# Four graph layers on one core: deferred loads, other turns, six exp buffers, and the MLP's second product by seven products

## The chip, the cores and the metric

The kernel runs on one core of one Trainium2 chip. The metric is the device time of one launch in microseconds (us), as a median over runs. The core's engines are named as in the profile: PE (TensorE, matrix products; PEld are its weight loads), DVE (VectorE), ACT (ScalarE), POOL (GpSimd), and SP (SyncE), which only issues DMAs here. Lines such as L521 are lines of the kernel before.

## The reference, cut to what matters

64 graphs of 256 nodes with 256 features pass four layers. After each layer the input is added and rows are normalised.

```python
# layer 0: 4 heads of 64, masked by adj
out = softmax(where(adj == 0, NEG, q @ k.T * 64**-0.5)) @ v
x = layernorm(x + layernorm(out @ Wo.T + bo) * gamma + beta)
# layer 1: 8 heads of 32 on the normalised rows themselves, then an MLP
normed = layer_norm(x, gamma1, beta1)
x1 = x + softmax(masked(normed @ normed.T * 32**-0.5)) @ normed
y = layer_norm(x1, gamma2, beta2)
x = layernorm(x + x1 + gelu(y @ W1 + b1) @ W2 + b2)      # W1 256x1024, W2 1024x256
# layer 2: scores from two vectors, leaky_relu, masked softmax, times x @ W
# layer 3: scores (x * a0) @ x.T, leaky_relu, masked softmax, times x
```

The product `gelu(...) @ W2` is the MLP's second product. Adjacency holds 0 and 1, is symmetric and has a full diagonal.

## The kernel before

The work runs in f32. `usual_input` does it all; at its end a flag tells whether the inputs had the properties that it relies on, and only if not, `any_input` computes everything again in a slower way. With these inputs it isn't entered.

**Groups and turns.** Two graphs are a group (G = 2, T = 512 rows), so there are 32 groups. `group(g)` is a generator: it loads x and adj, makes the mask, and runs layers 0 to 3; at each `yield` another generator may go on. The order of the program is that of the turns: the digits of `FIRST` name the groups that take the first turns; then, for each of 32 periods, the digits of `ORDER` name ages, where age a in period p is group p - a; the digits of `LAST` count back from the last group. In steady state groups of six ages are under way, and one leaves per period. `prepare`, which works out small constants (bop, the extra columns of wx, b2m, bounds), takes turns of its own beside group 0 from that group's turn `PREPARE` + 1 on.

**Engine order.** PE's instructions keep exactly the order of the program (`in_order` chains them). The other engines' instructions were set in an order of their own when the program was built; on the chip each engine runs its list in that order and waits for semaphores.

**What the steps put where.** Scores go into `ps` (PSUM, two buffers of 128x1024), ACT makes `e` by exp (L598), DVE multiplies by the mask (L600 for layer 0, L606 for layer 1, four of 256 columns for each e, with the row sums), PE multiplies e by the values (`pm<-e,v`, `pm<-e,z`). `e` has eight buffers. All other products go into `pm` (PSUM, four buffers of 128x512). Normalisation is bn_stats and bn_aggr on DVE (L537, L538), then two POOL instructions for the root (L540, L544), then DVE (L552). Layer 0 needs 1/sum along the other axis: `behind` writes zs to DRAM (`lines`, L719) and reads it back spread over partitions (`rr`, L721, two DMAs for each graph), all issued by SP; then DVE scales oT (L723), PE multiplies by WoT, and DVE's L730 and the norms follow, up to z. PE transposes z (L524) for layer 1.

**The MLP.** L779 is ACT's gelu into hT, laid out 128 x 8 x 512. `project` then computes, for each graph, a bias product (`b2m`, bf16, three rows that sum to b2 minus beta1) and, for both blocks of 128 rows, 8 matmuls with 128 rows of hT stationary and 256 columns of W2 moving; DVE's L692 adds `both` and takes the sum from PSUM into y. It yields after each block.

**Start.** SP issues, in this order: x and adj of group 0, WvT, WoT, the small constants, x and adj of group 1, W1, W2, adj of group 2, and then the first four DMA transposes (adjT, L888) that the mask (L891) needs. WqT, WkT, bq and bk are issued by ACT.

Of the kernel before, what the change touches and what calls it, by code (L numbers as in the profile page):

```python
# [8 lines left out]
F32 = mybir.dt.float32  # L9
# [4 lines left out]
ALU = mybir.AluOpType  # L14
AX = mybir.AxisListType

P = 128
N = 256
D = 256
NC = D // P  # L20
G = 2
QB = N // P
# [4 lines left out]
NF = DFF // P  # L27
# [6 lines left out]
AT_ONCE = 3  # L34


ORDER = "011225334342343542234235432323132121321132121"


FIRST = "3100000000021101000001010000010111"  # L40
LAST = ("001142322312324311231243212120210102100210100031121201213200120132101010010120100010101102"
        "01021000001000010010000")
PREPARE = 5

# [356 lines left out]
def usual_input(ctx: ExitStack, tc: tile.TileContext, a: dict, out: bass.AP, flag: bass.AP):  # L401
# [40 lines left out]
    def load_group(g):  # L442
        x0 = io.tile([P, TB, D], F32, name="x0")
        nc.sync.dma_start(x0, a["x"][g * G:(g + 1) * G].rearrange("b (q p) d -> p (b q) d", p=P))
        adj = io.tile([P, TB, N], I32, name="adj")
        nc.sync.dma_start(adj, a["adj"][g * G:(g + 1) * G].rearrange("b (q p) k -> p (b q) k", p=P))
        return x0, adj

    def load_rows(name, cols, queue=nc.sync):

        src = a[name]
        t = const.tile([P, src.shape[0] // P, cols], F32, name=name)
        queue.dma_start(t, src.rearrange("(c p) f -> p c f", p=P))
        return t

    def load_column(src, n, name, queue=nc.sync):

        t = const.tile([P, n // P], F32, name=name)
        queue.dma_start(t, src.rearrange("(c p) -> p c", p=P))
        return t  # L460

    setup = act.tile([P, NF, T], F32, name="setup", tag="hT", bufs=1).rearrange("p f t -> p (f t)")
# [1 line left out]
    def load_all(src, name, at=None):  # L464

        t = const.tile([P, D], F32, name=name) if at is None else setup[:, at:at + D]
        nc.sync.dma_start(t, src.unsqueeze(0).to_broadcast([P, D]))
        return t


    first = load_group(0)
# [1 line left out]
    wkT = load_rows("L0_gnn_WkT", D, nc.scalar)  # L473
    bq = load_column(a["L0_gnn_bq"], D, "bq", nc.scalar)
    bk = load_column(a["L0_gnn_bk"], D, "bk", nc.scalar)
    wvT = load_rows("L0_gnn_WvT", D)
    woT = load_rows("L0_gnn_WoT", D)
    bv = load_column(a["L0_gnn_bv"], D, "bv")
    bo = load_all(a["L0_gnn_bo"], "bo", 0)

    wx = const.tile([P, NC, D + 3], F32, name="wx")
    nc.sync.dma_start(wx[:, :, 0:D], a["L2_gnn_W"].rearrange("(c p) f -> p c f", p=P))
    a12 = setup[:, 768:1280].rearrange("p (s d) -> p s d", s=2)
    nc.sync.dma_start(a12, a["L2_gnn_a"].rearrange("(s f) o -> o s f", s=2).to_broadcast([P, 2, D]))
    beta0 = load_all(a["L0_gnn_beta"], "beta0")
    gamma0 = load_all(a["L0_gnn_gamma"], "gamma0")
    beta1r = load_all(a["L1_gnn_beta1"], "beta1r")
# [5 lines left out]
    beta2 = load_column(a["L1_gnn_beta2"], D, "beta2")  # L493
    b1 = load_column(a["L1_gnn_b1"], DFF, "b1")
    a0 = load_column(a["L3_gnn_a0"], D, "a0")
    second = load_group(1)
    w1 = load_rows("L1_gnn_W1", DFF)
    w2 = load_rows("L1_gnn_W2", D)

    wa1 = const.tile([P, 2, NC], F32, name="wa1")  # L500
    b2m = const.tile([P, D], BF16, name="b2m")
    onesb = const.tile([P, P], BF16, name="onesb")
# [17 lines left out]
    def matmul(*args, **kw):  # L520
        in_order(nc.tensor.matmul(*args, **kw))  # L521
# [60 lines left out]
    def scores(i, cs, qT, kT, mask, hd, scale, sums=None):  # L582

        m = P // hd
        es = []
        for c in cs:
            pss = [ps_s.tile([P, 2, QB * N], F32, name="ps") for _ in range(m // 2)]
            for kc in range(QB):  # L590
                for h in range(m):
                    r = h * hd
                    matmul(pss[h // 2][:, h % 2, kc * N:(kc + 1) * N],
                           kT[r:r + hd, c, i * N + kc * P:i * N + (kc + 1) * P],
                           qT[r:r + hd, c, i * N:(i + 1) * N], start=True, stop=True)
            for ps in pss:
                e = att.tile([P, 2, QB * N], F32, name="e", bufs=8)
                nc.scalar.activation(e, ps, AF.Exp, scale=scale)  # L598
                if sums is None:
                    nc.vector.tensor_tensor(e, e, mask.unsqueeze(1).to_broadcast([P, 2, QB * N]), ALU.mult)  # L600
                else:
                    for h in range(2):
                        for kc in range(QB):
                            k = slice(kc * N, (kc + 1) * N)
                            j = 2 * len(es) + h
                            nc.vector.scalar_tensor_tensor(e[:, h, k], e[:, h, k], 1.0, mask[:, k], ALU.mult, ALU.mult,  # L606
                                                           accum_out=sums[:, kc, c, j:j + 1])
                es.append(e)
        return es
# [63 lines left out]
    def project(dst, srcT, w, extra, row=None, gs=ALL):  # L673


        chunks = w.shape[1]
        for i in gs:
            pm = ps_m.tile([P, QB, D], F32, name="pm")
            if row is not None:
                matmul(pm, onesb, row.unsqueeze(1).to_broadcast([P, QB, D]), start=True, stop=False)  # L680
            for q in range(QB):
                t = i * QB + q
                for c in range(chunks):
                    matmul(pm[:, q, :], srcT[:, c, t * P:(t + 1) * P], w[:, c, :],
                           start=c == 0 and row is None, stop=c == chunks - 1 and (row is None or q == QB - 1))
                if chunks > NC:
                    yield
            o = dst[:, i * QB:(i + 1) * QB, :]
            if extra is None:
                nc.scalar.copy(o, pm)  # L690
            else:
                nc.vector.tensor_tensor(o, pm, extra[:, i * QB:(i + 1) * QB, 0:D], ALU.add)  # L692

    def layer0(g, x, mask):
        xT = transposed(x)
# [178 lines left out]
        return (yield from values_of(lambda i, kc, q: e[:, i, at[kc][q]:at[kc][q] + P], x, D, x, r_3[:, g], gs, last[:, g]))  # L874

    def group(g):
        x, adj = (first, second)[g] if g < 2 else load_group(g)
        yield
        adjb = io.tile([P, TB, N], BF16, name="adjb", bufs=1)
        nc.scalar.activation(adjb, adj, AF.Copy, accum_out=there[:, g:g + 1])  # L880
        nc.scalar.activation(adj.bitcast(F32), adj, AF.Square, bias=minus_half, accum_out=edges[:, g:g + 1])
        yield


        pt = io.tile([P, G, QB, N], BF16, name="adjT", bufs=1)
        for t in range(TB):
            i, q = divmod(t, QB)
            nc.sync.dma_start_transpose(pt[:, i, :, q * P:(q + 1) * P], adjb[:, t, :])  # L888
        yield
        mask = act.tile([P, G, QB * N], BF16, name="mask")  # L890
        nc.vector.scalar_tensor_tensor(mask.rearrange("p g k -> p (g k)"), pt.rearrange("p g k q -> p (g k q)"), 1.0,  # L891
                                       adjb.rearrange("p t k -> p (t k)"), ALU.mult, ALU.min,
                                       accum_out=both_ways[:, g:g + 1])
        xb, z = yield from layer0(g, x, mask)
        y, hT, both = yield from layer1(xb, z, mask)

        def others(gs):

            yield from project(y, hT, w2, both, b2m, gs)
# [12 lines left out]
        while parts:  # L912
            for r in parts[:turn // QB + 1]:
                if next(r, END) == END:
                    parts.remove(r)
            turn += 1
            yield

    def prepare():


        bvr = setup[:, 2560:2816].rearrange("p (c q) -> p c q", c=NC)
        nc.vector.tensor_copy(bvr, bv.unsqueeze(2).to_broadcast([P, NC, P]))
# [5 lines left out]
        yield  # L929
# [15 lines left out]
        for k in range(3):  # L945
            nc.vector.tensor_copy(part, left)
            nc.sync.dma_start(b2m[k:k + 1, :], part[0:1, :])
            if k < 2:
                nc.vector.tensor_tensor(left, left, part, ALU.subtract)

        yield

# [101 lines left out]
```

## Time and profile before

| | us |
|---|---|
| median of 10 runs (2661.74 to 2667.36) | 2665.37 |
| the profiled execution, its own time | 2668.45 |
| span of its instructions | 2666.6 |
| PE busy | 2591.1 |
| DVE busy | 1966.4 |
| ACT busy | 1293.2 |
| first mask (L891) starts at | 31.3 |
| mask to mask, from 217.9 to 2466.9 | 80.3 |

Durations below come from the one profiled execution. "Busy" is the union of an engine's instructions. A group line of the profile reads: line, engine, operation, written tile <- read tiles, shapes, count, then busy us and the mean ns of one, then the engine's idle time just before and what ended it. A timeline line reads: start, length, engine, line, operation, tiles, count, and in brackets the idle time before it. A product in f32 appears as two records on PE. Matmuls are pipelined, so the records of neighbours overlap, and the distance between starts is what they cost.

### The profile page before, as it was taken

To read this page: it belongs to the slowest core of one execution; us is meant where nothing else is said; L and a number is where in the kernel's file an instruction comes from. 1 tells how busy PE (TensorE), PEld (TensorE's weight loads), DVE (VectorE), ACT (ScalarE), POOL (GpSimd) and SP (SyncE) were. 2 spreads that over 40 slices of the span, in tenths; PEclk is the share of its full clock that TensorE was granted. 3 is DMA by queue.
4 is the path that set the end of the run, shared out by engine and by line. 5 is a ranking of instruction groups with operands and counts; after the bars stand their busy time and mean duration, and the time that the engine had idled before them with its cause. 6 is when DMAs were issued, how large, how long until landed. Compare 5 with 4: busy or idle time off the path is not lost.

```text
span 2666.6 us, 44866 instructions
## 1 busy us (share of the span) xinstructions
PE 2591.1 (97%) x16648; PEld 1767.3 (66%) x16648; DVE 1966.4 (74%) x6189; ACT 1293.2 (48%) x1995; POOL 587.5 (22%) x1139
## 2 busy tenths in 40 slices
PE   6899999999999999999999999999999999999996
PEld 3466667666666676666676666676676676676665
DVE  4667777777777777777777777777777777777774
ACT  3445545545544445545455545555444555444442
POOL 1112222212222212222222222222222222222221
PEclk8899999999999999999999999999999999999998
DMA  5001011100010110110110110010110110000000
GB/s 154 25 9 29 29 37 29 33 29 29 29 37 27 31 32 25 32 37 26 28 37 25 32 37 25 29 37 23 35 36 25 29 37 21 29 29 17 17 1 25
DMA packets 113728, 83.20 MB, mean 31 GB/s; under 512 B 44256, under 2 KB 113120, under 8 KB 113504
## 3 DMA queue, kind: packets, MB, share of 16 engines
q1 hardware_dynamic: 112416, 79.74, 10.1%
q8 instruction: 134, 2.20, 0.4%
q14 instruction: 90, 0.74, 0.1%
q10 hardware_dynamic: 1088, 0.53, 0.1%
HBM read 54.80 MB, written 17.04 MB: 27 GB/s over the span
## 4 chain that ended last, share of the span: by engine, by line
PE 72%; DVE 16%; POOL 8%; issue 2%; DMA 1%; SPq 1%; ACT 1%; DVEq 0%; ACTq 0%; POOLq 0%
PE pm L521 55%; PE ps L521 10%; PE pm L524 7%; POOL rstd L544 6%; DVE st L537 3%; DVE y L807 2%; DVE y L735 2%; DVE xn L552 2%; POOL ve L540 2%; DVE z L552 2%; DVE mv L538 1%; DVE y L734 1%; DVE xb L741 1%; DVE r L806 1%; SPq L888 1%
## 5 line engine op out<-in xcount | busy, mean ns | idle before, releaser
L606 DVE SCALAR_TENSOR_TENSOR e<-e,mask 128x256 f32<-128x256 f32 x1024 | 428.3, 485 | 130.0 <-ACT e L598 130.0
L598 ACT ACTIVATE e<-ps 128x1024 f32<-128x1024 f32 x384 | 372.2, 1021 | 197.5 <-PE ps L521 181.0
L521 PE MATMUL pm<-L_gnn_W,hT 128*128 128x256 f32 x2048 | 463.0, 379 | 0.0
L521 PE MATMUL pm<-xT,L_gnn_W 128*128 128x512 f32 x1024 | 455.8, 593 | 0.0
L521 PEld LDWEIGHTS pm<-L_gnn_W,hT 128*128 128x128 f32 x2048 | 384.5, 190 | 49.2 <-issue 0.7
L779 ACT ACTIVATE hT<-pm,b 128x512 f32<-128x512 f32 x256 | 177.2, 692 | 409.7 <-PE pm L521 409.7
L521 PEld LDWEIGHTS pm<-xT,L_gnn_W 128*128 128x128 f32 x1024 | 192.4, 191 | 204.0 <-issue 199.5
L537 DVE BATCH_NORM_STATS2 st<-y 128x6 f32<-128x256 f32 x768 | 301.8, 409 | 6.7
L544 POOL TENSOR_TENSOR rstd<-ve,mhalf 128x2 f32<-128x2 f32 (+1 forms) x384 | 298.0, 776 | 26.7
L552 DVE TENSOR_SCALAR xn<-y,mv,rstd 128x256 f32<-128x256 f32 x384 | 142.2, 412 | 177.4 <-POOL rstd L544 177.4
L540 POOL TENSOR_SCALAR ve<-mv 128x2 f32<-128x2 f32 x384 | 98.9, 258 | 757.7 <-DVE mv L538 757.2
L765 POOL TENSOR_TENSOR both<-y,xb 128x512 f32<-128x512 f32 x64 | 81.3, 1271 | 760.4 <-DVE y L764 760.4
L600 DVE TENSOR_TENSOR e<-e,mask 128x1024 f32<-128x1024 f32 x128 | 151.0, 1221 | 17.4 <-ACT e L598 17.4
L521 PE MATMUL ps<-xT 32*128 32x256 f32 x2048 | 151.8, 407 | 1.7 <-ACT e L598 1.5
L579 ACT ACTIVATE xT<-pm,beta,gamma 128x512 f32<-128x512 f32 x128 | 92.6, 771 | 113.3 <-PE pm L524 113.1
L521 PEld LDWEIGHTS ps<-xT 32*128 32x128 f32 x2048 | 95.0, 187 | 75.4 <-issue 66.4
L521 PE MATMUL pm<-e,z 128*32 128x256 f32 x2048 | 139.2, 387 | 0.1
L521 PE MATMUL pm<-L_gnn_WoT,oT 128*128 128x256 f32 x512 | 121.4, 391 | 13.2 <-DVE oT L723 13.2
L521 PE MATMUL pm<-e,v 128*32 128x256 f32 x2048 | 125.5, 386 | 5.6 <-DVE e L600 5.6
L521 PE MATMUL ps<-qT,kT 64*128 64x256 f32 x1024 | 128.0, 389 | 0.6 <-ACT e L598 0.6
L521 PE MATMUL pm<-xT,L_gnn_WqT 128*128 128x512 f32 x256 | 120.2, 613 | 3.4 <-ACT xT L577 3.4
L807 DVE SCALAR_TENSOR_TENSOR y<-pm,r,xn 128x256 f32<-128x256 f32 x256 | 121.2, 474 | 2.5
(136 smaller groups left out, 4064.5 us busy)
## 6 DMA issues: line engine op xcount, KB each, us to landing
x<-in_x SPq DMA_DIRECT2D x32, 512.0 KB
adj<-in_adj SPq DMA_DIRECT2D x32, 512.0 KB
rr<-lines SPq DMA_DIRECT2D x128, 128.0 KB
out<-xn SPq DMA_DIRECT2D x31, 512.0 KB
L_gnn_W<-in_L_gnn_W SPq DMA_DIRECT2D x2, 1024.0 KB
adjT<-adjb SPq DMA_TRANSPOSE x128
lines<-zs SPq DMA_DIRECT2D x64, 4.0 KB
out<-xn SPq DMA_DIRECT2D x2, 256.0 KB
```

Of the source, the lines that this page charges most:

```text
L521: in_order(nc.tensor.matmul(*args, **kw))
L524: in_order(nc.tensor.transpose(*args))
L537: nc.vector.bn_stats(st[:, q, :], src[:, t, 0:D])
L540: nc.gpsimd.tensor_scalar(ve[:, 0], mv[:, :, 1], EPS, None, ALU.add)
L544: nc.gpsimd.tensor_tensor(rstd, ve, mhalf[:, 0:k * QB].rearrange("p (k t) -> p k t", k=k), ALU.pow)
L552: nc.vector.tensor_scalar(dst[:, t, 0:D], src[:, t, 0:D], mv[:, q, 0:1], rstd[:, q:q + 1], ALU.subtract, ALU.mult)
L579: nc.scalar.activation(dst[:, c, on], pt[:, on], AF.Identity, bias=bias[:, c:c + 1], scale=scale[:, c:c + 1])
L598: nc.scalar.activation(e, ps, AF.Exp, scale=scale)
L600: nc.vector.tensor_tensor(e, e, mask.unsqueeze(1).to_broadcast([P, 2, QB * N]), ALU.mult)
L606: nc.vector.scalar_tensor_tensor(e[:, h, k], e[:, h, k], 1.0, mask[:, k], ALU.mult, ALU.mult, accum_out=sums[:, kc, c, j:j + 1])
L779: nc.scalar.activation(hT[:, f, :], pm, AF.Gelu, bias=b1[:, f:f + 1])
L807: nc.vector.scalar_tensor_tensor(y[:, t, :], po[:, 0:D], r, x[:, t, 0:D], ALU.mult, ALU.add)
```

## The change

**Seven products.** For every group but the last, `project` is replaced by `quarters` and `in_seven`. hT is taken as a 2 x 2 matrix of blocks (graph x half of the 1024), W2 as 2 x 2 (half of the 1024 x half of the columns). `quarters` forms three new sums of blocks in s1, s2 and s4 and one in place in hT; `prepare` forms four differences of W2's blocks once, in `wd`. Seven block products then take the place of eight, each 8 matmuls with 128 moving columns, accumulated in pa, px and py, and DVE adds them up in y. s1, s2 and s4 use the buffers of z, kT and qT.

**Loads.** What group 0's first steps don't need is put into the list `later` and issued on SP at the start of `prepare`. WvT goes to ACT's queue. Group 1 is loaded in its own turn.

**Turns and buffers.** FIRST, ORDER, LAST and PREPARE are other rows (36 first turns instead of 34; PREPARE 2 with four empty turns behind the loads). `e` has six buffers instead of eight.

```diff
-ORDER = "011225334342343542234235432323132121321132121"
-FIRST = "3100000000021101000001010000010111"
-LAST = ("001142322312324311231243212120210102100210100031121201213200120132101010010120100010101102"
-        "01021000001000010010000")
-PREPARE = 5
+ORDER = "001222533434324352334422132453233212211231312"
+FIRST = "000000110000021311001001010000001011"
+LAST = ("011142232321324122331102134212210110012020100031121210213011220010231011000011020010101020"
+        "11012000000100100010000")
+PREPARE = 2
...
+    later = []
+    def load(queue, to, of):
+        if queue:
+            queue.dma_start(to, of)
+        else:
+            later.append((to, of))
...
-    wvT = load_rows("L0_gnn_WvT", D)
+    wvT = load_rows("L0_gnn_WvT", D, nc.scalar)
...
-    second = load_group(1)
+    wd = const.tile([P, 4, NF // 2, P], F32, name="wd")
...
-                e = att.tile([P, 2, QB * N], F32, name="e", bufs=8)
+                e = att.tile([P, 2, QB * N], F32, name="e", bufs=6)
...
+    def quarters(hT):
+        a = [[hT[:, k * NF // 2:(k + 1) * NF // 2, i * N:(i + 1) * N] for k in range(2)] for i in range(G)]
+        s1 = act.tile([P, NF // 2, N], F32, name="s1", tag="z")
+        s2 = act.tile([P, NF // 2, N], F32, name="s2", tag="kT")
+        s4 = act.tile([P, NF // 2, N], F32, name="s4", tag="qT")
+        nc.vector.tensor_tensor(s1, a[1][0], a[1][1], ALU.add)
+        nc.vector.tensor_tensor(s2, s1, a[0][0], ALU.subtract)
+        nc.vector.tensor_tensor(a[1][0], a[0][0], a[1][0], ALU.subtract)
+        nc.vector.tensor_tensor(s4, a[0][1], s2, ALU.subtract)
+        return a, s1, s2, s4
+
+    def in_seven(dst, of, extra):
...
+        pa = ps_m.tile([P, QB, 2, P], F32, name="pm")
+        px = ps_m.tile([P, QB, 2, P], F32, name="pm")
+        product(pa[:, :, 0], a[0][0], quarter(0, 0))
+        w = att.tile([P, QB, P], F32, name="w", bufs=1)
+        nc.scalar.copy(w, pa[:, :, 0])
+        nc.vector.tensor_tensor(r1[:, :, 0], pa[:, :, 0], e1[:, :, 0], ALU.add)
+        matmul(px, onesb, rows, start=True, stop=False)
+        product(px[:, :, 0], a[1][1], wd[:, 3], False, False)
+        yield
+        product(px[:, :, 1], s1, wd[:, 0], False)
+        nc.vector.tensor_tensor(r2, px, e2, ALU.add)
+        nc.vector.tensor_tensor(r1[:, :, 1], px[:, :, 1], e1[:, :, 1], ALU.add)
+        product(pa[:, :, 1], s2, wd[:, 1])
+        nc.vector.tensor_tensor(w, w, pa[:, :, 1], ALU.add)
+        nc.vector.tensor_tensor(r1[:, :, 1], r1[:, :, 1], w, ALU.add)
+        yield
+        product(pa[:, :, 0], a[1][0], wd[:, 2])
+        nc.vector.tensor_tensor(w, w, pa[:, :, 0], ALU.add)
+        nc.vector.tensor_tensor(r2, r2, w.unsqueeze(2).to_broadcast([P, QB, 2, P]), ALU.add)
+        yield
+        py = ps_m.tile([P, QB, 2, P], F32, name="pm")
+        matmul(py[:, :, 0], onesb, rows[:, :, 0], start=True, stop=False)
+        product(py[:, :, 0], a[0][1], quarter(1, 0), False)
+        product(py[:, :, 1], s4, quarter(1, 1))
+        nc.vector.tensor_tensor(r1, r1, py, ALU.add)
+        yield
...
+        of = quarters(hT) if g < B // G - 1 else None
...
+            if len(gs) == G:
+                yield from in_seven(y, of, both)
+            else:
+                yield from project(y, hT, w2, both, b2m, gs)
...
     def prepare():
+        for to, of in later:
+            nc.sync.dma_start(to, of)
+        for _ in range(4):
+            yield
...
+        (b11, b12), (b21, b22) = ([w2[:, k * NF // 2:(k + 1) * NF // 2, n * P:(n + 1) * P] for n in range(2)] for k in range(2))
+        for k, (p, m) in enumerate(((b12, b11), (b22, wd[:, 0]), (b22, b12), (b21, wd[:, 1]))):
+            nc.vector.tensor_tensor(wd[:, k], p, m, ALU.subtract)
```

In the program built from it, on each engine in order: SP issues x and adj of group 0, seven of the deferred loads (WoT first), the four transposes of group 0, the other eleven (W1 and W2 last), then x and adj of group 1. On PE a period reads, from layer 3's transposes on: two transposes of x, the first product, the bias, the second product, the transposes of z, layer 3's scores, the products of s1 and s2, scores, the fifth product, the bias, the sixth and seventh, scores, `e,z`, WqT, scores, `e,z`, scores, `e,z`, transposes of oT, WkT, WvT, `e,z`, and then layer 0's scores and products as before.

More of the change, by code (lines that the diff above doesn't have):

```diff
@@ L447, in load_group, with load_rows, load_column @@
         return x0, adj
-    def load_rows(name, cols, queue=nc.sync):
+    later = []
[4 more added lines that the diff above has]
+            later.append((to, of))
+    def load_rows(name, cols, queue=None):
         src = a[name]
         t = const.tile([P, src.shape[0] // P, cols], F32, name=name)
-        queue.dma_start(t, src.rearrange("(c p) f -> p c f", p=P))
+        load(queue, t, src.rearrange("(c p) f -> p c f", p=P))
         return t
-    def load_column(src, n, name, queue=nc.sync):
+    def load_column(src, n, name, queue=None):
         t = const.tile([P, n // P], F32, name=name)
-        queue.dma_start(t, src.rearrange("(c p) -> p c", p=P))
+        load(queue, t, src.rearrange("(c p) -> p c", p=P))
         return t
@@ L466, in load_all @@
         t = const.tile([P, D], F32, name=name) if at is None else setup[:, at:at + D]
-        nc.sync.dma_start(t, src.unsqueeze(0).to_broadcast([P, D]))
+        load(None, t, src.unsqueeze(0).to_broadcast([P, D]))
         return t
@@ L481, in usual_input @@
     wx = const.tile([P, NC, D + 3], F32, name="wx")
-    nc.sync.dma_start(wx[:, :, 0:D], a["L2_gnn_W"].rearrange("(c p) f -> p c f", p=P))
+    load(None, wx[:, :, 0:D], a["L2_gnn_W"].rearrange("(c p) f -> p c f", p=P))
     a12 = setup[:, 768:1280].rearrange("p (s d) -> p s d", s=2)
-    nc.sync.dma_start(a12, a["L2_gnn_a"].rearrange("(s f) o -> o s f", s=2).to_broadcast([P, 2, D]))
+    load(None, a12, a["L2_gnn_a"].rearrange("(s f) o -> o s f", s=2).to_broadcast([P, 2, D]))
     beta0 = load_all(a["L0_gnn_beta"], "beta0")
@@ new lines, in in_seven, with product, quarter, part @@
+    def in_seven(dst, of, extra):
+        a, s1, s2, s4 = of
+        def product(to, s, w, start=True, stop=True):
+            for q in range(QB):
+                for c in range(NF // 2):
+                    matmul(to[:, q, :], s[:, c, q * P:(q + 1) * P], w[:, c, :], start=start and c == 0,
+                           stop=stop and c == NF // 2 - 1 and (start or q == QB - 1))
+        def quarter(k, n):
+            return w2[:, k * NF // 2:(k + 1) * NF // 2, n * P:(n + 1) * P]
+        def part(t, i):
+            return t[:, i * QB:(i + 1) * QB, 0:D].rearrange("p q (n d) -> p q n d", n=2)
+        r1, r2, e1, e2 = part(dst, 0), part(dst, 1), part(extra, 0), part(extra, 1)
+        rows = b2m.rearrange("p (n d) -> p n d", n=2).unsqueeze(1).to_broadcast([P, QB, 2, P])
+        pa = ps_m.tile([P, QB, 2, P], F32, name="pm")
[24 more added lines that the diff above has]
+        yield
@@ L876, in group @@
     def group(g):
-        x, adj = (first, second)[g] if g < 2 else load_group(g)
+        x, adj = load_group(g) if g else first
         yield
@@ L895, in group @@
         y, hT, both = yield from layer1(xb, z, mask)
+        of = quarters(hT) if g < B // G - 1 else None
         def others(gs):
-            yield from project(y, hT, w2, both, b2m, gs)
+            if len(gs) == G:
+                yield from in_seven(y, of, both)
+            else:
+                yield from project(y, hT, w2, both, b2m, gs)
             x = yield from renormed(y, gs)
@@ L927, in prepare @@
         nc.vector.tensor_tensor(bop, pm, bo, ALU.add)
-        yield
+        for _ in range(1):
+            yield
         wa = setup[:, 1280:2304].rearrange("p (s c d) -> p s c d", s=2, c=NC)
@@ L949, in prepare @@
                 nc.vector.tensor_tensor(left, left, part, ALU.subtract)
+        yield
+        (b11, b12), (b21, b22) = ([w2[:, k * NF // 2:(k + 1) * NF // 2, n * P:(n + 1) * P] for n in range(2)] for k in range(2))
+        for k, (p, m) in enumerate(((b12, b11), (b22, wd[:, 0]), (b22, b12), (b21, wd[:, 1]))):
+            nc.vector.tensor_tensor(wd[:, k], p, m, ALU.subtract)
         yield
```

## The prediction

> **What bounds the kernel now.** I read the page's busy line first, then its slices, then the groups of equal instructions, then two stretches of the timeline. Busy line and slices:
>
> ```profile
> PE 2591.1 (97%) x16648; PEld 1767.3 (66%) x16648; DVE 1966.4 (74%) x6189; ACT 1293.2 (48%) x1995; POOL 587.5 (22%) x1139
> ...
> PE   6899999999999999999999999999999999999996
> PEld 3466667666666676666676666676676676676665
> ```
>
> PE is full from slice 3 to 39; only the ends are not. The view by windows gives PE and DVE for the start, one period and the tail (span, then PE busy, its records, PEld, DVE, ACT, POOL):
>
> ```profile
> 0.00:100.00 100.00, 67.25 (x408) 39.77 (x412) 49.83 (x156) 40.44 (x61) 14.40 (x31) 0.83 0.42 108
> 1338.50:1418.80 80.30, 79.95 (x521) 54.72 (x520) 61.06 (x192) 40.28 (x62) 18.28 (x36) 1.00 0.11 31
> 2467.00:2667.00 200.00, 174.52 (x994) 122.92 (x992) 129.12 (x433) 72.68 (x121) 38.05 (x87) 0.94 0.04 14
> ```
>
> The mask instruction (L891) recurs every 80.30 us from 217.9 to 2466.9 us: 28 periods, one group each, PE-bound. A microsecond of PE per period is worth 28 us; DVE has 19 us to spare per period.
>
> A busy PE is not PE at its peak, so I price matmuls by start-to-start distance. Timeline, PE alone (start, us, engine, line, tiles, count):
>
> ```profile
> 1332.22 2.78 PE L521 MATMUL ps<-z,xT 128*128 128x256 f32 x16
> 1334.84 0.38 PE L521 MATMUL pm<-b2m,onesb 128*128 128x512 bf16 x1
> 1335.06 3.62 PE L521 MATMUL pm<-L_gnn_W,hT 128*128 128x256 f32 x16
> 1338.51 0.38 PE L524 MATMUL pm<-ident,z 128*128 128x128 f32 x2
> ```
>
> An f32 matmul is two records. 16 records of 256 columns take 1335.06 to 1338.51: 0.216 us each. The row above holds 8 of 256 and 8 of 128 columns in 2.62 us: (2.62 - 8 x 0.216) / 8 = **0.111 us for 128 columns**, each with its own weight load.
>
> [...] The trace shows single loads of 190 ns, but in runs of 128-column matmuls they follow each other at 111 ns[...]. [...] the trace has 1222 (L836). [...]
>
> **Seven products.** Per group, 32 matmuls of 256 columns were 64 records x 0.216 = 13.82 us, bias 2 x 0.216. Now 7 products x 8 = 56 matmuls of 128 columns: 112 x 0.111 = 12.43 us, bias 0.216 + 0.108. Saved: 1.50 us per group, on the path, in 31 of 32 groups (the last keeps `project`). Bounds of the pace: half of 0.216 (0.108) and the unoverlapped load (0.190).
>
> DVE gains four f32 sums of 1024 (`quarters`): 4 x 1.22 = 4.88 us. Evictions were 2 x 0.69; now three of 512 (0.69) and five of 256 (0.42): 4.17. Net +7.7 us: 61.1 becomes 68.8 of about 79 us, 87%. It lies beside PE; its cover is DVE's slack, and it comes bunched. ACT's added copy (256 columns, 0.37) is hidden: ACT works 40 of 80 us.
>
> The new waits on PE, from the order in the built program: product three waits for s1, four for s2, five for `w` plus the fourth (its tile is reused). I walk the stretch from the z transposes' end (0): DVE xb to 0.1, s1 1.3, r1 1.7, s2 2.9, the two other sums 5.3, px's evictions 6.4, layer 3's maximum 7.4, w 7.8. PE: layer 3's scores to 2.7, s1's product 4.5, s2's 6.3, next scores 7.3, then w at 7.9: 0.6 late or less. Then DVE: layer 3's mask 8.8, r1 9.2, the next group's mask 10.4, first e x mask four 11.8, w 12.3, the next four 13.8. PE: 9.7, bias and two products 13.4, scores 14.3, then e,z. **About half a microsecond spare.** Queued behind the sums are the mask (adjb on ACT waits for it, and the second exp behind that) and the eight e x mask that PE's e,z needs. Loss 0 to 1.2; I take 0.4.
>
> **The turns (ORDER).** Two moves count. W1's last four and layer 3's score matmuls change places with the first two products, so z meets PE almost on time: before, PE stood at the z transposes 0.8 us a period (16.6 us over 21 periods, by start-to-start distances). And WkT moves behind the third e,z, so that scores, e,z, scores, e,z follow each other with nothing between. The tail shows the price:
>
> ```profile
> 2554.55 1.07 PE L521 MATMUL pm<-e,z 128*32 128x256 f32 x16
> 2555.73 0.70 PE L521 MATMUL ps<-xT 32*128 32x256 f32 x4
> 2556.65 1.13 PE L521 MATMUL ps<-xT 32*128 32x256 f32 x12 [0.22 <-ACT e L598]
> 2557.71 1.62 PE L521 MATMUL pm<-e,z 128*32 128x256 f32 x16
> ```
>
> Scores to the next e,z's end took 3.53 us (2555.73 to 2559.26) against 2.06 unhindered (0.99 + 1.07): 1.5 us, as two PSUM tiles and exps of 1.02 us set the pace. Period: 80.3 - 1.5 - 0.6 (of z's 0.8) + 0.4 + 1.5 - 0.6 (small score and e,z waits that were there already) = **79.5**; one transition fewer between tilings of the array (0.09), and the walk, carried on through the rest of the period in the same way, closes at 78.5: I take the middle, **79.0**. Bounds 77.9 and 80.5. Times 28: -36 us.
>
> **Six buffers of exp.** Costed at nothing: each exp's slot was last read by an e,z or e,v that stands ahead of its own scores on PE, so PE covers it; if not, an exp comes late by at most one e,z (1.07). Bounds 0 to +0.5 a period, inside those above.
>
> **Start.** On SP the four adjT transposes were 25th to 28th, behind all constants and two groups' loads: first mask at 31.3. Now they are 10th to 13th, so the mask can come at 18 to 20. But DVE's two pairs of differences for `wd` stand ahead of the first e x mask, and need W2, now SP's 20th load: transposes' issue until about 16, nine small loads at 0.5 each, then W1 and W2, 2 MB at some 0.37 MB/us (the rate at 22 to 28 us): 28 to 31. With 2.8 us of differences the first e,v starts at 32 to 35.5 instead of 33.96: nothing gained there (bounds -2 and +2). WvT on ACT's queue (issue 0.5) lands before its use at 20 us; the second group's x, now the 21st and issued in its own turn, is wanted after 40. `prepare` starts at group 0's third turn, issues the deferred loads, W1 and W2 last (all on SP, none on POOL), and then stands four turns; its product for bop (0.86 us on PE) now follows WvT, so it no longer holds WvT up, and its three b2m copies stay ahead of the second group's transposes, as before.
>
> Behind it, PE stood here:
>
> ```profile
> 33.96 3.64 PE L521 MATMUL pm<-e,v 128*32 128x256 f32 x32 [5.55 <-DVE e L600]
> ...
> 48.95 3.42 PE L521 MATMUL pm<-L_gnn_WoT,oT 128*128 128x256 f32 x8 [6.03 <-DVE oT L723]
> 57.95 3.75 PE L521 MATMUL pm<-L_gnn_WoT,oT 128*128 128x256 f32 x8 [5.58 <-DVE oT L723]
> ```
>
> The second WoT half waited because SP issued a third group's transposes (5.07) between the two graphs' rr loads. Now both `lines` and four rr go together, behind one set of transposes: -5. Group 1's WqT is put into the first WoT wait (3.6 us of work), and WkT, WvT and scores ahead of the z transposes, which stood 3.5: -3.6 and -2, less 1.5 for layer 1's scores that lose WvT as filler. Sum **-9**, bounds -3 and -15. The first two groups' seven products: -3.
>
> **Tail.** One group with seven products lies in it (-1.5), and the W2 piece that filled one of its score gaps is gone (+1.5): 0, bounds -6 and +6.
>
> **Sum.** Span: -36 - 9 - 3 = -48. The profiled execution took 2668.45 (span 2666.6 and 1.85 around it), 3.1 above the median 2665.37. 2668.45 - 48 = 2620.5; less 3.1, a median of **2617 us**.
>
> **The rivals.** (1) Hand-overs and exps fit: period 77.9, 28 x -2.4 - 12 = -79: 2586. For it: DVE's slack on average; against: the measured 1.5. (2) The saving is eaten: the gaps of the new turns and late evictions return 1.5 us, period 80.3, only the start gains 12: 2653. For it: PE idles wherever a DVE result is due within 0.5 us. (3) **Slower: DVE's queue between z and the first e,z.** Its slack is half a microsecond; if sums and evictions run 1 to 2 us later than walked (dependent sums not overlapping, PSUM tiles held longer), PE stands at the fifth product and again at e,z. It decides from 1.7 us beyond my walk per period: at 80.7 the 28 periods give back the start's 12. At 2.5, period 81.5: +34 - 12, 2687. Against it: 68.8 of 81 us is no full engine. (4) Weight loads don't overlap in long runs: 112 x 0.190 = 21.3 us, +7.4 a group with the bias, times 31, less 9: about 2885. Against it: the runs of four at 0.111.
>
> **How the numbers follow.** Forecast 0.56 (own range 2600 to 2642), (1) 0.12, (2) 0.19, of which 0.04 within 0.2% of before (about what a measurement of this kernel can tell from no change), (3) 0.10, (4) 0.03. Faster 0.56 + 0.12 + 0.15 = 0.83, same 0.04, slower 0.13. The range 2590 to 2660 leaves out (3), (4) and the edges.
>
> **What would show it.** Steps right: mask to mask 79.0; W2 and wd records 0.111 apart; DVE near 83% of the span; PE idle before the z transposes under 0.3 and about 1.5 between second scores and third e,z; first e,v still at 32 to 35.5, WoT's second half without a wait of 5. Wrong: a period of 80.3 or more with DVE as releaser ahead of the wd or e,z matmuls (2 or 3), 0.19 between wd records (4), a first e,v before 30.

## The result, and the profile after

| | before | after |
|---|---|---|
| median, us | 2665.04 (2661.62 to 2667.36) | 2730.6 (2727.28 to 2733.99) |
| ratio | | 1.0248, 95% interval 1.0239 to 1.0257 |
| span of the profiled execution, us | 2666.6 | 2730.7 |
| steady period, us | 80.32 | 82.64 |

The change made the kernel slower by 2.5%; 2617 us was forecast. Lines below are those of the kernel after (L710 of before is L777 now, L521 is L529, L546 is L554). The accounting is short: measured at PE's z transposes, the fifth group stands 3.6 us later than before (378.3 against 374.7), the 27 periods from there to the last group take 60.1 us more (2228.8 against 2168.7), and the tail behind is 0.4 us longer (123.6 against 123.2). Together 64.1, the difference of the spans. **The loss is in the period.**

The page of the kernel after: the busy line, and the slices of PE and of its granted clock.

```profile
PE 2616.6 (96%) x18136; PEld 1812.8 (66%) x18136; DVE 2175.4 (80%) x6503; ACT 1306.5 (48%) x2026; POOL 587.1 (21%) x1139
...
PE   6899999999999999999999999999999999999996
...
PEclk8999999999999999999999999999999999999998
```

PE is as full as before, DVE went from 74 to 80%, POOL's work did not change. By windows (start, one period from mask to mask, tail; columns as in the prediction):

```profile
0.00:100.00 100.00, 70.06 (x454) 40.92 (x454) 53.42 (x162) 41.83 (x62) 14.28 (x30) 0.88 0.42 108
1381.92:1464.12 82.20, 80.60 (x570) 56.08 (x569) 67.39 (x203) 40.74 (x64) 18.28 (x35) 1.00 0.11 30
2530.73:2730.70 199.97, 173.23 (x1082) 123.73 (x1080) 139.79 (x454) 74.45 (x123) 35.29 (x87) 0.97 0.04 14
```

In one period PE's idle time grew from 0.35 us (80.30 less 79.95, before) to 1.60 (82.20 less 80.60), and the view doesn't say where. The reading starts at PE's timeline where it stands longest, the z transposes:

```profile
1364.17 1.04 PE L532 MATMUL pm<-ident,x 128*128 128x128 f32 x8
1365.31 2.05 PE L529 MATMUL pm<-L_gnn_W,hT 128*128 128x128 f32 x16
1367.19 0.38 PE L529 MATMUL pm<-b2m,onesb 128*128 128x512 bf16 x1
1367.41 1.95 PE L529 MATMUL pm<-wd,hT 128*128 128x128 f32 x16
1369.97 0.56 PE L532 MATMUL pm<-ident,z 128*128 128x128 f32 x2 [0.61 <-DVE z L560]
1371.32 1.41 PE L532 MATMUL pm<-ident,z 128*128 128x128 f32 x6 [0.79 <-DVE z L560]
```

The 16 W2 records take (1367.19 - 1365.31) / 16 = 0.117 us each, the joint included: the seven products run nearly as forecast. But two waits for z follow, 0.61 and 0.79. z comes from DVE, so DVE's timeline of the same stretch is next:

```profile
1364.97 0.16 DVE L554 TENSOR_TENSOR rstd<-rstd 128x2 f32<-128x2 f32 x1 [1.39 <-POOL rstd L552]
...
1366.99 2.31 DVE L554 TENSOR_TENSOR rstd<-rstd 128x2 f32<-128x2 f32 x1 [1.66 <-POOL rstd L552]
1369.34 0.16 DVE L555 TENSOR_TENSOR rstd<-rstd,ve 128x2 f32<-128x2 f32 x1
1369.42 0.73 DVE L560 TENSOR_SCALAR z<-y,mv,rstd 128x256 f32<-128x256 f32 x2
```

The same instruction, two elements a partition, takes 0.16 us for one graph and 2.31 for the other. POOL's timeline says what ran meanwhile:

```profile
1365.94 1.03 POOL L552 TENSOR_TENSOR rstd<-ve,mhalf 128x4 f32<-128x4 f32 x1
1366.93 2.35 POOL L777 TENSOR_TENSOR x<-x,beta 128x1024 f32<-128x1024 f32 x1
```

L777 is layer 0's `x + beta0` for the next group. It waits for that group's x transposes, and the new turns put these ahead of the z transposes (1364.17). So POOL starts it at once behind L552, its instruction for the root, which releases L554; and L554 ends 0.02 us behind L777. Over the run, as minimum, median and maximum in ns:

```profile
L554 DVE TENSOR_TENSOR rstd<-rstd x64: 160/163/2320, 73.2 to 2606.0; 128x2 f32<-128x2 f32 x64
```

**The kernel before showed it already, in a place where it cost nothing.** There POOL's add ran 11 us behind the root (L544, until 1338.6), and it held the last of eight e x mask; first DVE, then POOL, of the kernel before:

```profile
1349.38 0.43 DVE L606 SCALAR_TENSOR_TENSOR e<-e,mask 128x256 f32<-128x256 f32 x1
...
1349.72 2.57 DVE L606 SCALAR_TENSOR_TENSOR e<-e,mask 128x256 f32<-128x256 f32 x1
```

```profile
1349.60 2.42 POOL L710 TENSOR_TENSOR x<-x,beta 128x1024 f32<-128x1024 f32 x1 [2.97 <-PE pm L524]
```

PE's `e,z` of that graph follows its scores at 1353.97 without a wait. A group line's mean (485 ns) hides the hold: in 30 of the 32 groups one record of about 2.57 stands among 31 of about 0.42.

Both held instructions started behind the add, L554 by 0.06 us and the e x mask by 0.12, and ended 0.02 and 0.27 behind its end: 2.31 us for 0.16, and 2.57 for 0.43. In after, 30 of the 32 groups have such an L554 (2.31 or 2.32). Both read two tensors; that this decides is a guess, which a run below tries.

### The profile page after: what moved, and what is told of

It reads as the page before. It is cut to its first block, busy times and chain, and to the rows that moved or that the text cites. A ratio compares the mean times of both kernels' runs of the same rounds, so it can differ in the third digit from the quotient of the medians.

```text
span 2730.7 us, 48187 instructions
## 1 busy us (share of the span) xinstructions
PE 2616.6 (96%) x18136; PEld 1812.8 (66%) x18136; DVE 2175.4 (80%) x6503; ACT 1306.5 (48%) x2026; POOL 587.1 (21%) x1139
## 4 chain that ended last, share of the span: by engine, by line
PE 47%; DVE 32%; POOL 12%; issue 3%; ACT 2%; DMA 2%; SPq 1%; POOLq 0%; DVEq 0%; ACTq 0%
PE pm L529 31%; PE ps L529 12%; POOL rstd L552 8%; DVE st L545 4%; DVE zs L642 4%; PE pm L532 3%; POOL ve L548 3%; DVE y L874 3%; DVE xn L560 3%; DVE rstd L554 3%; ACT e L606 2%; DVE y L802 2%; DVE mv L546 2%; DVE qT L901 2%; DVE qT L903 1%
## 5 line engine op out<-in xcount | busy, mean ns | idle before, releaser
L529 PE MATMUL pm<-xT,L_gnn_W 128*128 128x512 f32 x1024 | 454.8, 597 | 0.5
L614 DVE SCALAR_TENSOR_TENSOR e<-e,mask 128x256 f32<-128x256 f32 x1024 | 364.1, 421 | 69.3 <-ACT e L606 69.2
L529 PEld LDWEIGHTS pm<-xT,L_gnn_W 128*128 128x128 f32 x1024 | 192.0, 190 | 225.3 <-issue 192.0
L552 POOL TENSOR_TENSOR rstd<-ve,mhalf 128x2 f32<-128x2 f32 (+1 forms) x384 | 298.3, 777 | 26.6
L560 DVE TENSOR_SCALAR xn<-y,mv,rstd 128x256 f32<-128x256 f32 x384 | 161.6, 468 | 111.4 <-POOL rstd L552 111.4
L529 PE MATMUL ps<-xT 32*128 32x256 f32 x2048 | 170.2, 405 | 11.3 <-ACT e L606 8.0
L529 PE MATMUL pm<-e,z 128*32 128x256 f32 x2048 | 159.0, 386 | 0.3
L554 DVE TENSOR_TENSOR rstd<-rstd 128x2 f32<-128x2 f32 x64 | 74.8, 1168 | 97.6 <-POOL rstd L552 97.6
L529 PEld LDWEIGHTS ps<-xT 32*128 32x128 f32 x2048 | 102.1, 185 | 75.3 <-ACT e L606 40.4
L529 PE MATMUL pm<-L_gnn_W,hT 128*128 128x128 f32 (+1 forms) x1056 | 138.2, 284 | 2.7
L529 PE MATMUL ps<-qT,kT 64*128 64x256 f32 x1024 | 129.1, 391 | 6.9 <-ACT e L606 6.9
L529 PEld LDWEIGHTS pm<-L_gnn_W,hT 128*128 128x128 f32 x1056 | 127.6, 192 | 11.7 <-ACT z L914 9.7
L529 PE MATMUL pm<-e,v 128*32 128x256 f32 x2048 | 125.7, 386 | 2.3 <-DVE e L608 2.3
L529 PEld LDWEIGHTS pm<-wd,hT 128*128 128x128 f32 x992 | 117.9, 192 | 11.4 <-DVE w L747 8.3
L529 PE MATMUL pm<-L_gnn_WoT,oT 128*128 128x256 f32 x512 | 118.6, 386 | 6.9 <-DVE oT L790 6.9
```

The source lines that it names most:

```text
L552: nc.gpsimd.tensor_tensor(rstd, ve, mhalf[:, 0:k * QB].rearrange("p (k t) -> p k t", k=k), ALU.pow)
L554: nc.vector.tensor_tensor(rstd[:, 0], rstd[:, 0], rstd[:, 1], ALU.mult)
L560: nc.vector.tensor_scalar(dst[:, t, 0:D], src[:, t, 0:D], mv[:, q, 0:1], rstd[:, q:q + 1], ALU.subtract, ALU.mult)
```

## The experiments

"P" in the expectations is the theory that POOL's add holds DVE on the way to z; "Q" is the prediction's rival 3, DVE's sums and evictions. Where PE's time per period is split below, it is by the distance from each record's start to the next, over 20 periods.

### The add left out, and the add moved

```diff
 e1_no_add, against after
-        nc.gpsimd.tensor_tensor(x, x, over_blocks(beta0), ALU.add)
 e2_add_moved, against after
-        nc.gpsimd.tensor_tensor(x, x, over_blocks(beta0), ALU.add)
...
         def behind(i, oT, rz):
+            if i == 0:
+                added = nc.gpsimd.tensor_tensor(x, x, over_blocks(beta0), ALU.add)
+                if len(rstds) > 20:
+                    tc.add_manual_dep(added.ins, rstds[-1], ...)   # same engine: an order, no wait
```

> The kernel after without POOL's x + beta0 (2.35 us once a group; beta0 is left out of layer 0, the rest stays). Theory P (POOL's add holds DVE's two-element product rstd*rstd on the way to z): that product falls from 2.31 to about 0.16 us, z is ready 2.1 us sooner in every period, PE's stand at the z transposes falls from about 2.0 us to under 0.3 and the half-clock stretches with it; period from 82.7 to 80.0-80.8, the whole 2650 to 2680 us. Rival Q (DVE's quarter sums and evictions and the adjacency of scores and e,z set the period): POOL's add is beside them, the period stays within 0.5 of 82.7, the whole 2715 to 2731 us.

> The kernel after with the same x + beta0 put 40 us later in POOL's queue (behind layer 1's rstd of the first graph), where DVE stands idle for some 2 us. Theory P: as good as leaving the add out, within 0.3%: period 80.0-80.9, the whole 2650 to 2685 us. Theory Q: 2715 to 2731 us. If it is POOL's work as such and not its place that costs, the time stays at the kernel after's.

Without the add: 2662.56 us, ratio to before 0.9995 (0.9986 to 1.0003), period 80.27. With the add moved: 2665.23, ratio 1.0005 (0.9996 to 1.0014), period 80.28. P holds and Q falls (its adjacency of scores and e,z is real, but costs less than this, as shown below): 68 and 65 us of the loss are the place of one POOL instruction, not its work. L554 in e1:

```profile
L554 DVE TENSOR_TENSOR rstd<-rstd x64: 160/161/164, 72.5 to 2537.0; 128x2 f32<-128x2 f32 x64
```

One detail of e2's expectation was wrong: DVE was not idle there. The add holds layer 1's last xb instead (two of 0.40 take 2.80), and nothing on PE waits for that xb at this place. A hold costs what PE waits behind it: 0.01 us a period here (80.28 against 80.27), 2.37 at z in after (82.64 against 80.27).

### The same add, DVE's instruction with one tensor input

```diff
-            nc.vector.tensor_tensor(rstd[:, 0], rstd[:, 0], rstd[:, 1], ALU.mult)
-            nc.vector.tensor_tensor(rstd[:, 0], rstd[:, 0], ve[:, 1], ALU.mult)
+            for q in range(QB):
+                nc.vector.tensor_scalar(rstd[:, 0, q:q + 1], rstd[:, 0, q:q + 1], rstd[:, 1, q:q + 1],
+                                        ve[:, 1, q:q + 1], ALU.mult, ALU.mult)
```

> The kernel after with POOL's x + beta0 in its place, but the two products that mend rstd written as one tensor_scalar for each block of tokens, with the two factors as scalars: one tensor input instead of two. Theory [...]: these take 0.1 to 0.3 us beside the running add, period 80.0 to 80.9, the whole 2650 to 2685 us; the next two-input instruction of DVE (xb) may be held instead, up to the add's end. Rival: any instruction of DVE that reads SBUF is held by POOL's add: 2.3 us as before, 2720 to 2735 us.

2722.34 us, ratio 1.0221 (1.0206 to 1.0237), period 82.31: the time that the rival gives, but not by its mechanism. DVE, then POOL, of e8_one_input:

```profile
1279.47 0.46 DVE L555 TENSOR_SCALAR rstd<-rstd,ve 128x1 f32<-128x1 f32 x2 [1.71 <-POOL rstd L552]
1279.84 2.39 DVE L561 TENSOR_SCALAR z<-y,mv,rstd 128x256 f32<-128x256 f32 x2
```

```profile
1279.41 2.35 POOL L778 TENSOR_TENSOR x<-x,beta 128x1024 f32<-128x1024 f32 x1
```

The one-input instructions passed beside the running add (0.46 for both); then z, also one tensor input but 256 columns, was held to the add's end (2.07 for the first, 0.40 for the second). So a hold doesn't need two tensor inputs, and the guess falls. The rival's mechanism, that any DVE instruction reading SBUF is held, is refuted by the tail of e10, an experiment told below. There two bn_stats of 256 columns, one input each, pass beside the add, and the first `tensor_scalar` of 256 columns is held to its end (1.66); DVE, then POOL:

```profile
2474.73 0.75 DVE L546 BATCH_NORM_STATS2 st<-y 128x6 f32<-128x256 f32 x2
2475.40 2.99 DVE L562 TENSOR_SCALAR xn<-y,mv,rstd 128x256 f32<-128x256 f32 x2
```

```profile
2474.41 2.50 POOL L781 TENSOR_TENSOR x<-x,beta 128x1024 f32<-128x1024 f32 x1 [9.80 <-ACT kT L773]
```

What sets z and xn (unhindered 0.40 and 0.41 us) apart from the instructions that passed was not shown; the number of columns alone doesn't, since bn_stats passed with 256. For the fix this is enough: another form of the product only passes the hold on to z, and moving the add (e2) removes it.

### Which part of the change: turns, or seven products

```diff
 e3_turns_only, against before: ORDER and LAST of after
 e4_old_turns, against after: ORDER and LAST of before
 e6_no_seven, against e2_add_moved
-        of = quarters(hT) if g < B // G - 1 else None
...
-            if len(gs) == G:
-                yield from in_seven(y, of, both)
-            else:
-                yield from project(y, hT, w2, both, b2m, gs)
+            yield from project(y, hT, w2, both, b2m, gs)
```

> The kernel before with the new row of turns (ORDER and LAST) alone: the MLP's second product as before, eight buffers of exp, its own loads and FIRST. Theory P: the new turns put x's transposes ahead of z's, and POOL's add behind z's rstd, so it falls on the same two-element product; the period is the kernel after's plus the 1.5 us that seven products save, 83.5 to 84.5, the whole 2745 to 2790 us. Theory Q (the seven products' work on DVE is what costs): period 79 to 80.3, the whole 2630 to 2665 us.

> The kernel after with the old row of turns (ORDER and LAST of before; seven products, deferred loads, FIRST and six buffers stay). Theory P: x's transposes and POOL's add come behind the z chain again; the period is the old one less what seven products save, 78.8 to 80.0 if their waits stay small, the whole 2610 to 2655 us. Theory Q: the sums and evictions sit in the old turns too, period 81 to 83, the whole above 2690 us.

> The kernel of e2_add_moved with the second product of the MLP as in the kernel before for all groups (no quarters, no seven products; turns, loads and six buffers stay). Theory: the seven products are worth what their records say, 1.2 us of PE per group: period 81.3 to 81.7, the whole 2690 to 2710 us. Rival: DVE's 7.7 us more per group take back what PE saves: period 80.0 to 80.6, 2655 to 2675 us.

**The turns alone:** 2797.91 us, ratio 1.0484 (1.0451 to 1.0518), period 85.33. The direction is P's, the size is not: the period is 0.8 us above its range. In every period of the profiled execution from 381 us on, a stretch of 3.41 us with the clock at a half follows the stand at z and lengthens layer 3's scores from 2.62 to 3.98; its mean granted clock is 0.972, before's 0.988. That execution was the slowest of four (2785.07 to 2809.94).

**Seven products in the old turns:** 2913.56 us, ratio 1.0931 (1.0913 to 1.095), period 88.77. P's forecast of 2610 to 2655 is refuted, and Q's of more than 2690 came true, for this order of turns. PE of e4_old_turns:

```profile
1455.37 1.16 PE L532 MATMUL pm<-ident,z 128*128 128x128 f32 x6 [0.16 <-DVE z L560]
1457.69 2.05 PE L529 MATMUL pm<-wd,s 128*128 128x128 f32 x16 [1.16 <-DVE s L709]
1463.36 3.79 PE L529 MATMUL pm<-wd,s 128*128 128x128 f32 x16 [3.62 <-DVE y L739]
```

The old turns put the third and fourth product right behind the z transposes. There DVE has z, xb, four sums, layer 3's maximum and masks, and the evictions in one queue, and PE waits for s1, then for a PSUM tile. The second product takes 18.83 us a period instead of 13.22; of the difference about 1.8 is that the 16 records from 1463.36 ran while the granted clock was at a half (for 6.83 us from 1461.8): 3.71 us to the next start, against 1.83 for 16 of the same records in after (32 from 1376.53 to 1380.19). So of these two orders only the new one carries the seven products: rival 3's mechanism exists, only not in the kernel after. POOL's add holds an e x mask here too (2.58 at 1472.12); whether it has a share in the 1.3 us that scores and e,z lose against e1 was not tried.

**New turns, add out of the way, no seven products:** 2699.96 us, ratio 1.0134 (1.0119 to 1.015), period 81.55 against 80.28 of e2. The seven products are worth **1.27 us a period**, the theory's 1.2, and DVE's additional work costs PE nothing there. With the second product as before, the new turns thus cost 81.55 - 80.32 = 1.23 us a period even with the add out of the way.

### The price of the turns: WkT back between the scores

In e1 and e2 layer 1's scores and e,z take 1.62 us more per period than before.

```diff
 e5_wkt_back, against e2_add_moved
-ORDER = "001222533434324352334422132453233212211231312"
+ORDER = "001222533434324352334422132453233212121231312"
```

> The kernel of e2_add_moved with one pair of turns changed back: WkT's product between the third and the fourth scores of layer 1, as in the kernel before. In e2 the score and e,z matmuls of layer 1 take 1.6 us more per period than in the kernel before. Theory: that is the price of four scores in a row on two PSUM tiles; with WkT between them 0.7 to 1.2 us of it come back, period 79.1 to 79.6, the whole 2630 to 2648 us. Rival: the wait only moves to the next e,z or to the scores of layer 0, period 80.1 to 80.4, 2660 to 2668 us.

2714.05 us, ratio 1.0188 (1.0174 to 1.0202), period 81.92: slower, though the theory's gain is there. Scores 5.21 to 4.30, e,z 4.73 to 4.00, WkT 3.44 to 3.63: -1.43, within 0.01 of the kernel before's values. Layer 0's scores and e,v lost 3.09. The add again, in DVE's and POOL's timeline of e5_wkt_back:

```profile
1318.00 2.76 DVE L562 TENSOR_SCALAR xb<-y,mv,rstd 128x256 f32<-128x256 f32 x2 [1.14 <-POOL rstd L553]
1320.68 1.21 DVE L610 TENSOR_TENSOR e<-e,mask 128x1024 f32<-128x1024 f32 x1
```

```profile
1317.94 2.35 POOL L786 TENSOR_TENSOR x<-x,beta 128x1024 f32<-128x1024 f32 x1
```

It holds the same xb as in e2, but layer 0's first e x mask now stands right behind, and e,v waits for it. Two runs test that reading, one without the add, and one where it waits for ACT's first half of k:

```diff
 e9_wkt_no_add, against e5: the add is left out
 e10_add_behind_k, against e5: the add goes back to its old place in the program, with a wait
+                if w is wkT and f == 0:
+                    k_half = made.ins.name          # made: ACT's activation into kT
...
+        added = nc.gpsimd.tensor_tensor(x, x, over_blocks(beta0), ALU.add)
+        tc.add_manual_dep(added.ins, k_half, ...)   # ACT to POOL: a semaphore
```

> The kernel of e5_wkt_back with POOL's x + beta0 left out (beta0 is left out of layer 0). In e5 the scores and e,z of layer 1 gave back 1.4 us per period as expected, but POOL's add had come to lie on layer 1's last xb, 2.4 us, and layer 0's scores and e,v lost 3.1. Theory: the loss is the add's place alone; without it the period is 78.9 to 79.5, the whole 2623 to 2642 us. Rival: WkT in its old place leaves layer 0's first scores too little time for their exps and masks whatever POOL does: period 80 to 82, 2655 to 2714 us.

> The kernel of e5_wkt_back with the add kept, and made to wait for ACT's copy of the first half of k, which comes where DVE stands idle for 2.9 us. Theory: within 0.3% of e9_wkt_no_add, 2623 to 2648 us, and faster than the kernel before by 0.6 to 1.5%. Rival: it meets the e x mask of layer 1 there and the period stays above 80: 2655 us or more.

e9: 2645.81 us, ratio 0.993 (0.9915 to 0.9945). e10: 2650.47, ratio 0.9947 (0.9933 to 0.996). Both have a period of 79.72. The add's place is again the cause, and e10 computes everything and is faster than both kernels. Both lie above their ranges, by 3.8 and 2.5 us, with a period 0.2 above e9's range: layer 0's first scores and e,v keep a wait of 0.88 a period. DVE and POOL of e10_add_behind_k:

```profile
1354.10 0.42 DVE L616 SCALAR_TENSOR_TENSOR e<-e,mask 128x256 f32<-128x256 f32 x1
...
1357.38 0.42 DVE L616 SCALAR_TENSOR_TENSOR e<-e,mask 128x256 f32<-128x256 f32 x1 [2.85 <-ACT e L608]
```

```profile
1354.30 2.43 POOL L781 TENSOR_TENSOR x<-x,beta 128x1024 f32<-128x1024 f32 x1 [5.95 <-ACT kT L773]
```

The add fits into DVE's wait for the next exp, and the e x mask on either side keep their 0.42.

### The start

PE, then ACT, of the kernel after:

```profile
27.56 1.13 PE L529 MATMUL ps<-qT,kT 64*128 64x256 f32 x8 [0.26 <-ACT e L606]
35.37 2.08 PE L529 MATMUL ps<-qT,kT 64*128 64x256 f32 x8 [6.67 <-ACT e L606]
37.37 3.57 PE L529 MATMUL pm<-e,v 128*32 128x256 f32 x32
...
44.93 1.07 PE L529 MATMUL pm<-e,v 128*32 128x256 f32 x16 [2.26 <-DVE e L608]
...
59.05 6.46 PE L529 MATMUL pm<-L_gnn_WoT,oT 128*128 128x256 f32 x16 [6.89 <-DVE oT L790]
```

```profile
26.49 1.02 ACT L606 ACTIVATE e<-ps 128x1024 f32<-128x1024 f32 x1 [1.35 <-PE ps L529]
33.25 1.06 ACT L947 ACTIVATE adjb<-adj 128x1024 bf16<-128x1024 int32 x1 [5.74 <-DMA b2m<-setup]
...
34.31 1.00 ACT L606 ACTIVATE e<-ps 128x1024 f32<-128x1024 f32 x1
```

The first e,v begins at 37.37, not at 32 to 35.5, and not for want of DVE alone: on ACT the second group's conversion of adj (L947) stands between two exps. Its adj is loaded behind all deferred loads.

```diff
 e7_prepare_later, against e2_add_moved: DVE's wd, b2m and the masks of groups 1 and 2
 are ordered behind group 0's fourth e x mask
+        for _ in range(6):
+            yield
...
+        behind_masks(nc.vector.tensor_tensor(left, b2, beta1r, ALU.subtract))
 e11_with_start, against e10_add_behind_k: the same, and ACT's L947 of group 1 behind group 0's exps
-FIRST = "000000110000021311001001010000001011"
+FIRST = "000000100001021311001001010000001011"
...
+            tc.add_manual_dep(copied.ins, exps[3], ...)
```

> The kernel of e2_add_moved with the differences of W2, b2m's three copies and the masks of the second and third group put behind the first group's four e x mask in DVE's queue. Theory (DVE's queue at the start holds the first group's e,v): first e,v at 29 to 31 us instead of 37.4, third and fourth without the wait of 2.3; the whole 3 to 7 us below e2, 2658 to 2662 us. Rival: the rr loads or the z chain of the first group take it back: 2664 to 2667 us.

> The kernel of e10_add_behind_k with the start of e7_prepare_later, and with ACT's conversion of the second group's adjacency behind the first group's four exps (in e7 the third and fourth exp stood behind it, which waited for its load, until 34 us). Theory: first e,v at 29 to 31 us, 3 to 9 us less than e10. Rival: the first group's rr loads set the start, as the second wait in e7: 0 to 3 us less than e10.

e7: 2662.99 us, ratio 0.9998 (0.999 to 1.0007). Its first e,v stayed at 37.0, behind a wait of 7.5 for ACT's exp, so the theory missed; the second e,v lost its wait, and the span is 2.8 us below e2's (2660.6 against 2663.4), less than these two ratios can tell apart. e11: 2645.33 us, ratio **0.993** (0.9916 to 0.9943), 5.1 below e10, as its theory had it. PE of e11_with_start:

```profile
27.48 2.06 PE L537 MATMUL ps<-qT,kT 64*128 64x256 f32 x16 [0.26 <-ACT e L615]
29.46 1.93 PE L537 MATMUL pm<-e,v 128*32 128x256 f32 x32
...
50.18 1.96 PE L537 MATMUL pm<-L_gnn_WoT,oT 128*128 128x256 f32 x8 [1.07 <-DVE oT L806]
57.18 3.75 PE L537 MATMUL pm<-L_gnn_WoT,oT 128*128 128x256 f32 x8 [5.03 <-DVE oT L806]
```

The first e,v came 7.9 us sooner than in after; WoT's second half again has the wait of 5 that it had before the change, so part of that is given back.

### Six buffers of exp

```diff
-                e = att.tile([P, 2, QB * N], F32, name="e", bufs=8)
+                e = att.tile([P, 2, QB * N], F32, name="e", bufs=6)
```

> The kernel before with six buffers of exp instead of eight, and nothing else. The prediction's step (PE covers it): 2660 to 2668 us, the kernel before's time. Rival: an exp comes late by part of one e,z each period (up to 0.5 us): up to 2682 us.

2664.1 us, ratio 1.0 (0.9991 to 1.0009): nothing, as the prediction had it.

## Why the prediction was wrong

PE's time per period, us, from start to start:

| | before | after | e1, no add | e10 |
|---|---|---|---|---|
| second product and bias | 14.45 | 13.86 | 13.22 | 13.22 |
| z transposes | 1.67 | 2.31 | 0.88 | 0.88 |
| layer 3's scores | 2.62 | 2.92 | 2.62 | 2.62 |
| layer 1's scores and e,z | 8.31 | 9.94 | 9.94 | 8.30 |
| x and ex transposes | 1.36 | 1.80 | 1.80 | 1.80 |
| WkT | 3.63 | 3.44 | 3.44 | 3.63 |
| layer 0's scores and e,v | 7.36 | 7.36 | 7.36 | 8.24 |
| the rest | 40.92 | 41.01 | 41.01 | 41.03 |
| period | 80.32 | 82.64 | 80.27 | 79.72 |

- **The step that failed: "Two moves count" (the turns).** Three did. The x transposes moved ahead of the z transposes, and POOL's add with them. The prediction followed PE and DVE through the move but not POOL's queue. It forecast z's stand to shrink by 0.6; without the add it shrinks by 0.79, with it the stand grows. The add's cost is after less e1: 1.43 at z, 0.64 at the wd records ahead of z (PE's wait shows in the distance to the next record), 0.30 in layer 3's scores at half clock: **2.37 us a period**.
- **The second failed term: -0.6 for "small score and e,z waits that were there already", and the half microsecond of averaging with the walk.** They had nothing behind them: in a steady period of the kernel before each of the four score runs takes 1.08 us from start to start and each of the four e,z 1.00, which is the 8.31 already; and with WkT back in its place they return to 8.30. Without the add the period would have been 80.27, not 79.0, and the gain nil. That is rival 2's outcome (saving eaten, 80.3), which had 0.19.
- **Seven products: right in kind, 1.50 forecast, 1.23 (e1) to 1.27 (e6) measured.** 32 records cost 3.67 us, 0.115 each with the joints between runs, not 0.111. Rival 4 (0.190) is out.
- **Adjacency, +1.5:** 1.62 in scores and e,z, less 0.20 in WkT; e5 gave back 1.43. The price read from the tail was good.
- **New waits, +0.4:** the place was wrong, and the size right by luck. s1, s2 and w cost nothing measurable in e1 (wd,s records at 0.115). Instead 0.44 came at the x and ex transposes; it belongs to the turns, since e6 has it without the seven products. Its cause was not followed further.
- **DVE, +7.7 a period, hidden:** its 1.22 us for a sum of 1024 columns held (1.22 to 1.23 for the four from 1372.29 in after). Over one period DVE is busy 65.6 us in e1 against 61.1 before, of which 2.1 was the held e x mask; so about 6.7 were added, and e6 shows that they are hidden.
- **Six buffers 0, tail 0:** right (e12; 123.6 against 123.2 behind the last z transposes). The tail's two halves of 1.5 were not measured apart.
- **Start, -9, and first groups, -3:** in e1, free of the add, the fifth group's z transposes come 3.1 us earlier than before (371.6 against 374.7), a quarter of it. W2's differences came when forecast (30.1), but ACT's queue was not walked: L947 waited for a load that had moved behind all deferred ones.
- **Rival 3 was on the right side, with the wrong place.** It named DVE's queue between z and e,z; the wait is ahead of z. Its mechanism is real in e4, where the seven products stand in the old turns.

## What to carry to other kernels

When a step moves, list everything it releases on every queue, and ask what runs on DVE at the moment POOL's long two-input instruction starts; here a two-element instruction of 0.16 us took 2.31, nearly the whole length of the add (2.35). Look in the profile before for single records far above their group's mean (2.57 among 0.42): in before they held up nothing on PE, and the new order put such a hold on the path, at 2.37 us a period. Let a long POOL instruction wait for an event that DVE idles after, as e10 does (79.72 us a period, against 81.92 in e5), rather than for the first moment at which it may run.

## What was not expected of the hardware

- POOL's 128x1024 add (2.35 us) held these DVE instructions that started behind it until 0.02 to 0.27 us past its end: a two-input product of 2 columns (0.16 to 2.31 us, after), e x mask (0.43 to 2.57, before), and `tensor_scalar` of 256 columns (0.40 to 2.07, e8). It did not hold `tensor_scalar` of one column (0.46 for two, e8) or bn_stats of 256 columns (0.75 for two, e10).
- The granted clock fell to a half for 3.41 us in 5 steady periods of after, each time behind PE's two waits for z. From 1371.9 us it came behind waits of 0.61 and 0.79 (PE was busy for 2.01 of the 3.41 us ahead of it), and layer 3's scores took 4.01 us instead of 2.62. What sets it off was not shown: waits of 0.80 and 0.78, from 708.9 us on, left the clock at 1.00, and the scores took 2.62. Before and e1 had no such stretch in a steady period, e3 in each from 381 us on, and in these profiled executions e3's period of 85.33 us is 25 times 3.413 (the length of that stretch in after's trace, to the nanosecond), e4's of 88.77 within 0.03 of 26 times. That the period settles on a multiple of this length is an observation of two kernels; its cause was not tried.
